# Graph rows as plain float32 of 256 columns in a graph block kernel

## The chip, the cores and the metric

The kernel runs on one core of a Trainium2 chip. The metric is the device time of one execution in microseconds. A core has five engines, each with its own queue of instructions, in order: TensorE (PE in the profile, with the loads of its stationary side shown as PEld), VectorE (DVE), ScalarE (ACT), GpSimd (POOL) and SyncE (SP, which here only issues DMA transfers). TensorE multiplies a stationary tile (up to 128 x 128) with a moving tile (up to 512 columns) into PSUM; VectorE and ScalarE read PSUM and write SBUF.

## The reference

There are 6250 nodes with 256 features and 200,000 edges sorted by destination. Cut to what matters here:

```
xn  = layernorm(x)
# graph convolution, with a self-loop for each node
h   = xn @ W
deg = number of edges into a node, plus 1;  dinv = 1 / sqrt(deg)
gnn = relu(segment_sum(h[src] * dinv[src] * dinv[dst], dst) + b)
# linear attention and a two-layer network on xn
mix = attention_block(xn)
x   = x + gnn + mix
# eight experts of 977 slots each, a token goes to its best expert
out = x + experts(layernorm(x))
```

The graph part can be written with rows g = dinv * h. For a node n it is relu(dinv[n] * (g[n] + the sum of g[s] over all edges s -> n) + b). The row g[n] is the self-loop, called the own row below.

## The kernel before

**Tiles.** The nodes lie in 49 tiles of 128 rows (the last has 106). The rows g of all 49 tiles are held in SBUF in `tabs` (`table`, `rows_of`, `source`, lines 128 to 145) and are also stored in DRAM as `g_dram`. Each row is kept in two parts of type float32r, 256 columns each: a first part written by ScalarE (`table_row`, line 475) and the rest, which VectorE computes as value minus first part (`table_rest`, line 481). So a row has 512 columns and 2 KB. float32r is float32 in size; TensorE multiplies it in another way than plain float32.

**First passes.** `first_passes` goes over pairs of tiles (`twos`), computes the normed x, its products and the attention's sums, and the rows g. Beside it `first_chain` searches in the sorted edges, finds degrees and builds the edge lists. Until the degrees are known (`dinv`), h is put back in the place of x (line 908); `late_rows` (line 485) turns these into rows g later, with `table_row` on ScalarE and `table_rest` on VectorE. `store_rows` (line 468) issues the transfers to `g_dram` on SP's queue. x is loaded at the start into SBUF that the tables take over later; from pair 20 on it is loaded a second time (`XIN`, line 60).

**The graph's sums** are made in two ways, each for a part of the 49 destination tiles.

- *Dense* (`dense`, line 1152), 32 tiles (`DTS`). For a destination tile u a matrix of edge counts A (source by destination, 49 blocks of 128 x 128) is built: VectorE makes one-hot rows (`onehots`, line 1134), TensorE multiplies them in bfloat16 (line 1177), ScalarE evicts the counts from PSUM into A as uint8 (lines 1181 and 1184). Then ScalarE widens five blocks of A at a time to float32r (`widened`, line 1165), and TensorE multiplies each block with the rows of its source tile into the PSUM tile `ps_d` (line 1199). This goes in 11 steps for a tile: the counts of tile u are built in the same steps in which those of tile u - 1 are multiplied (in steps 1 to 10, with 4 or 5 blocks each). There is one `ps_d`.
- *Gathered* (`gather`, line 1224), 17 tiles (`GTS`) with 33 groups of 128 edges each, 561 in all. GpSimd gathers the 128 source rows of a group from `g_dram` by an indirect DMA (line 1230), `LAG` = 7 groups ahead into `GB` = 9 buffers; VectorE makes a one-hot of the destinations (line 1245); TensorE multiplies it with the rows into `ps` (line 1256).

Edges that exceed the lists' room lie in one more tile of rows (`left`), which is added with a matmul for each destination tile (lines 1196 and 1255). The own row is added by a matmul of the identity with the row itself (lines 1195 and 1253), the first into its PSUM tile. At the end of a tile `put_sum` (ScalarE, line 1121) writes dinv times the first 256 columns, and `put_rest` (VectorE, line 1126) adds dinv times the other 256.

**Rounds.** `rounds` (line 1344) takes the pairs of tiles through the attention block, adds bias (`add_bias`, line 1384), the graph's sum and x, and does the routing. A finished pair is put into a slot tile (`to_slot`, line 1387; three buffers) and scattered to the experts' rows by GpSimd (line 1337).

**Order.** The three run as generators under an order written out by hand (lines 1704 to 1742): for each of 363 steps one step of `dense`, then steps of `rounds` and of `gather` at fixed rates. The order of instructions in each engine's queue is set by this and does not depend on times. After that the eight experts run (lines 1804 to 1838), in plain float32.

## Time and profile before

| | |
|---|---|
| three runs | 1502.11, 1503.97, 1504.27 us (median 1503.97) |
| the profiled execution | 1500.01 us |
| its span, first to last instruction | 1498.2 us |
| mean granted TensorE clock | 0.979 |
| TensorE busy | 1397.7 us (93%) |
| VectorE busy | 1004.2 us (67%) |
| ScalarE busy | 900.1 us (60%) |
| GpSimd busy | 745.3 us (50%) |
| DMA | 267.52 MB, mean 179 GB/s |

The page gives busy times over the span, then 40 equal slices of it with a digit for the busy share in tenths. A line of a group reads: source line, engine, operation, written tile <- read tiles, shapes, number of instructions | busy us, mean ns of one | idle time of the engine just before them, and who ended it. Busy time counts overlapping instructions once, so it can be less than number times mean. A line of a window reads: stretch, its length, busy time of each engine with the number of instructions, granted clock, DMA share and GB/s. A line of waits reads: who <- for whom: us in total, times, the longest. A line of the timeline reads: start, length, engine, group, number.

### The profile page before, as it was taken

How to read it: one execution, taken by the hardware profiler on the slowest of the kernel's cores; microseconds unless marked ns; L12 is line 12 of the kernel's file. 1: busy time of each engine (PE TensorE's matmuls, PEld its weight loads, DVE VectorE, ACT ScalarE, POOL GpSimd, SP SyncE). 2: the span in 40 equal slices, each digit the busy share in tenths (PEclk: the TensorE clock that was granted, in tenths of full speed). 3: DMA queues.
4: the chain of work that ended last, by engine and by line, in shares of the span. 5: the costliest groups of instructions: out<-in, count | busy, mean ns of one | idle time of the engine just before them, and what ended most of it. 6: DMA issues, size and time to landing. Idle time of an engine off the chain costs nothing. (4 is left out here: it accounts for less than half of the span.)

```text
span 1498.2 us, 22383 instructions
## 1 busy us (share of the span) xinstructions
PE 1397.7 (93%) x7002; PEld 1020.9 (68%) x7002; DVE 1004.2 (67%) x3435; ACT 900.1 (60%) x2051; POOL 745.3 (50%) x725
## 2 busy tenths in 40 slices
PE   5998997999998999999999989999997999999996
PEld 2665664777776777777776767767775767766854
DVE  6787696678887887878888878888865322222322
ACT  2776564677776777677776767777674333333321
POOL 0101542777776677777766677777661201111111
PEclk9999998999999999999999999999998999999998
DMA  8438675877787777877777777777765343333130
GB/s 266 144 124 275 195 233 172 225 198 201 188 219 207 180 201 211 223 200 214 204 202 205 196 192 202 186 209 210 182 170 171 120 149 110 127 129 132 47 109 11
DMA packets 173459, 267.52 MB, mean 179 GB/s; under 512 B 26409, under 2 KB 73984, under 8 KB 173318
## 3 DMA queue, kind: packets, MB, share of 16 engines
q0 software_dynamic: 89168, 166.39, 42.7%
q1 hardware_dynamic: 83268, 98.39, 19.9%
q10 hardware_dynamic: 882, 1.05, 0.3%
q8 instruction: 65, 1.06, 0.3%
q14 instruction: 76, 0.62, 0.1%
HBM read 208.05 MB, written 60.39 MB: 179 GB/s over the span
## 5 line engine op out<-in xcount | busy, mean ns | idle before, releaser
L1230 POOL DMA_INDIRECT gt<-g_dram,idxc x561 | 592.9, 1057 | 217.1 <-PE ps L1256 79.7
L1199 PE MATMUL ps_d<-tab,A_r 128*128 128x512 f32 x1568 | 425.8, 401 | 10.2 <-ACT A_r L1165 9.9
L1199 PEld LDWEIGHTS ps_d<-tab,A_r 128*128 128x128 f32 x1568 | 292.7, 190 | 88.6 <-ACT A_r L1165 26.5
L1181 ACT CAST A<-bp 128x294 uint8<-128x294 f32 x640 | 237.2, 430 | 186.9 <-PE bp L1177 185.4
L1165 ACT CAST A_r<-A 128x640 fp32r<-128x640 uint8 (+1 forms) x320 | 230.7, 723 | 6.6 <-PE ps_d L1199 5.0
L1256 PE MATMUL ps<-gt,oh 128*128 128x512 f32 x561 | 220.4, 451 | 2.5 <-DVE oh L1245 2.5
L1177 PE MATMUL bp<-hi,lo 128*128 128x147 bf16 x1408 | 187.3, 264 | 22.0 <-DVE hi L1134 13.1
L1177 PEld LDWEIGHTS <-lo 128*128 128x128 bf16 x1408 | 105.0, 105 | 123.0 <-issue 49.3
L1838 POOL DMA_INDIRECT out<-rep,who x43 | 42.5, 989 | 279.4 <-DVE rep L1835 225.5
L1804 PE MATMUL hpf<-xet,w1e 128*128 128x128 f32 (+3 forms) x576 | 159.2, 434 | 8.2 <-ACTq L1916 3.5
L1134 DVE TENSOR_TENSOR lo<-rowb,two 128x512 bf16<-128x512 bf16 x352 | 147.4, 419 | 21.0 <-PE bp L1177 13.6
L1134 DVE TENSOR_TENSOR hi<-hib,two 128x592 bf16<-128x592 bf16 x352 | 161.5, 459 | 0.0
L1814 PE MATMUL ypf<-w2e,hm 128*128 128x256 f32 (+1 forms) x688 | 151.4, 379 | 0.0
L1814 PEld LDWEIGHTS ypf<-w2e,hm 128*128 128x128 f32 (+1 forms) x688 | 128.8, 188 | 21.6 <-issue 2.6
L1245 DVE TENSOR_TENSOR oh<-rowb,rel 128x256 fp32r<-128x256 bf16 x281 | 116.2, 414 | 40.8 <-PE ps L1256 40.2
L1804 PEld LDWEIGHTS hpf<-xet,w1e 128*128 128x128 f32 x576 | 92.6, 198 | 66.4 <-issue 55.7
L1806 ACT ACTIVATE hm<-hpf,fb_s 128x128 f32<-128x128 f32 (+3 forms) x144 | 72.3, 513 | 87.6 <-PE hpf L1804 84.8
L1816 DVE TENSOR_TENSOR y<-ypf,fb_s 128x256 f32<-128x256 f32 (+1 forms) x43 | 18.2, 423 | 130.6 <-PE ypf L1814 130.6
L1256 PEld LDWEIGHTS ps<-gt,oh 128*128 128x128 f32 x561 | 97.2, 195 | 7.9 <-DVE oh L1245 3.4
L1817 ACT ACTIVATE y<-y,xe 128x256 f32<-128x256 f32 (+1 forms) x43 | 21.8, 508 | 124.8 <-DVE y L1816 124.8
L892 PE MATMUL mm<-wqkv_s,xnt 128*128 128x512 f32 (+1 forms) x196 | 93.4, 599 | 0.3 <-DVE tab L481 0.3
L1337 POOL DMA_INDIRECT xbuf<-slot,put x46 | 48.0, 1044 | 58.2 <-issue 29.5
(376 smaller groups left out, 1993.3 us busy)
## 6 DMA issues: line engine op xcount, KB each, us to landing
g_dram<-tab SPq DMA_DIRECT2D x24, 512.0 KB
xbuf<-zeros SPq DMA_DIRECT2D x26, 384.0 KB
gt<-g_dram,idxc POOLq DMA_INDIRECT x561, 3.8
w1e<-in_fw SPq DMA_DIRECT2D x8, 1024.0 KB
w2e<-in_fw SPq DMA_DIRECT2D x8, 1024.0 KB
xe<-xbuf SPq DMA_DIRECT2D x7, 1028.0 KB
xt<-in_x SPq DMA_DIRECT2D x28, 256.0 KB
xe<-xbuf SPq DMA_DIRECT2D x9, 771.0 KB
```

What stands on the lines that cost most here:

```text
L892: nc.tensor.matmul(kp[:r, :], xnt[:, c, i * r:i * r + r], wqkv_s[:, c, D:3 * D], start=(c == 0), stop=(c == 1))
L1134: V.tensor_tensor(one.rearrange("p g (w t) -> p g w t", t=2), row.rearrange("p (w t) -> p w t", t=2).unsqueeze(1).to_broadcast([P, 4, w // ...
L1165: nc.scalar.copy(o[:, :s1 - s0, :], mats[u][:, s0:s1, :])
L1177: nc.tensor.matmul(both[:, :, h * GN:(h + 1) * GN], lo[:, 2 * i + h, :], hi[:, 2 * i + h, :NB * GN].rearrange("p (s k) -> p s k", k=GN), s ...
L1181: nc.scalar.copy(mats[uu][:, :, GN * g:GN * (g + 2)], both)
L1199: nc.tensor.matmul(acc_ps, A[:, hi - s0, :], source(hi), start=False, stop=(hi == NB - 1))
L1230: nc.gpsimd.indirect_dma_start(out=gt, out_offset=None, in_=g_dram, in_offset=bass.IndirectOffsetOnAxis(ap=idxs[j // P][:, j % P:j % P + 1 ...
L1245: V.tensor_tensor(oh, rowb.unsqueeze(1).to_broadcast([P, 2, P]), rel[:, m:m + 2].unsqueeze(2).to_broadcast([P, 2, P]), op=OP.is_equal)
L1256: nc.tensor.matmul(ps, ohs.pop(i), tiles.pop(i), start=False, stop=(e == EB - 1))
L1804: nc.tensor.matmul(hp[:, :nn], w1e[:, c, f * P:(f + 1) * P], xet[:, c, at:at + nn], start=(c == 0), stop=(c == 1))
L1806: nc.scalar.activation(hm[:, f, :nn], hp[:, :nn], AF.Relu, bias=fb1_s[:, e * 8 + f:e * 8 + f + 1])
L1814: nc.tensor.matmul(yp[:r, :], hm[:, f, (i - i0) * P:(i - i0) * P + r], w2e[:, f, :], start=(f == 0), stop=(f == FF - 1))
```

## The change

Rows g are kept as plain float32 in one part of 256 columns. So `tabs` and `g_dram` have half the size and a gathered row has 1 KB. Every graph matmul takes plain float32 operands on both sides and 256 moving columns. ScalarE evicts the counts as float32, and the matmuls read them where they were written; `widened` goes. The identity matmuls go; `put_sum` is an addition by VectorE of the PSUM tile and the own row, for the dense tiles at the start of the next tile's first step, and the factor dinv moves into `add_bias`. `table_rest` goes; in `late_rows` the second tile of a pair is done by VectorE. The gather has 12 buffers and a lag of 9, the slots have 5 buffers, x is not loaded a second time, and the SBUF places of the tables and of x are dealt out anew. The path for inputs that do not fit the lists (under `flag == 1`) is changed likewise; it does not run on these inputs.

```diff
-GB = 9
-LAG = 7
+GB = 12
+LAG = 9
...
-XIN = 20
...
-    g_dram = dram.tile([N_NODES, 2 * D], F32, name="g_dram")
+    g_dram = dram.tile([N_NODES, D], F32, name="g_dram")
...
-            where = (3, 4, 5, 0, 1, 2, 6)[k]
-            tabs[k] = big.tile([P, min(8, NB - 8 * k), 2 * D], FR, name="tab", tag=f"T{where}")
+            where = (6, 0, 7, 1, 2, 3, 8)[k]
+            tabs[k] = big.tile([P, min(8, NB - 8 * k), D], F32, name="tab", tag=f"T{where}")
...
     def table_row(t, h):
 
         r = rows(t)
-        o = rows_of(t, 1)[:, 0, :]
-        nc.scalar.activation(o[:, :D], h, AF.Copy, scale=dinv[:r, t:t + 1])
-
-    def table_rest(t, h):
-
-        r = rows(t)
-        o = rows_of(t, 1)[:, 0, :]
-        V.scalar_tensor_tensor(o[:, D:], h, dinv[:r, t:t + 1], o[:, :D].bitcast(F32), op0=OP.mult, op1=OP.subtract)
+        nc.scalar.activation(rows_of(t, 1)[:, 0, :], h, AF.Copy, scale=dinv[:r, t:t + 1])
...
             for i in range(n):
-                table_row(t0 + i, x_in(t0 + i, 1)[:, 0, :])
-            yield
-            for i in range(n):
-                table_rest(t0 + i, x_in(t0 + i, 1)[:, 0, :])
+                t, h = t0 + i, x_in(t0 + i, 1)[:, 0, :]
+                if i:
+                    V.tensor_scalar(rows_of(t, 1)[:, 0, :], h, dinv[:, t:t + 1], None, op0=OP.mult)
+                else:
+                    table_row(t, h)
             store_rows(t0, n)
+            yield
...
-                if direct:
-                    table_rest(t0 + i, kp[:r, D:])
...
+    ma = tables.enter_context(tc.tile_pool(name="ma", bufs=2))
...
-            nc.scalar.activation(sums[gi][:r, t % 2, :], ps[:r, :D], AF.Copy, scale=dinv[:r, t:t + 1])
-
-        def put_rest(t, ps):
-            r = rows(t)
-            o = sums[t // 2][:r, t % 2, :]
-            V.scalar_tensor_tensor(o, ps[:r, D:], dinv[:r, t:t + 1], o, op0=OP.mult, op1=OP.add)
+            V.tensor_add(sums[gi][:r, t % 2, :], ps[:r], source(t)[:r])
             there.add(t)
...
-            def widened(u, p):
-
-                s0, s1 = share(p)
-                o = parts[p] = de.tile([P, 5, P], FR, name="A_r", tag="A_r")
-                nc.scalar.copy(o[:, :s1 - s0, :], mats[u][:, s0:s1, :])
...
                 for p in range(half):
+                    if rest is not None:
+                        put_sum(*rest)
+                        rest = None
                     if p == 1:
                         counted()
                     if u >= 1 and p >= 1:
 
                         if p == 1:
-                            acc_ps = dps.tile([P, 2 * D], F32, name="ps_d", tag="ps_d")
-                            nc.tensor.matmul(acc_ps, identr, source(DTS[u - 1]), start=True, stop=False)
-                            nc.tensor.matmul(acc_ps, ohl, left, start=False, stop=False)
-                        A, (s0, s1) = parts.pop(p), share(p)
-                        for hi in range(s0, s1):
-                            nc.tensor.matmul(acc_ps, A[:, hi - s0, :], source(hi), start=False, stop=(hi == NB - 1))
+                            acc_ps = dps.tile([P, D], F32, name="ps_d", tag="ps_d")
+                            nc.tensor.matmul(acc_ps, ohl, left, start=True, stop=False)
+                        for hi in range(*share(p)):
+                            nc.tensor.matmul(acc_ps, mats[u - 1][:, hi, :], source(hi), start=False, stop=(hi == NB - 1))
                     if u < ND:
                         if p == 0:
-                            mats[u] = de.tile([P, NB, P], U8, name="A", tag="A")
+                            mats[u] = ma.tile([P, NB, P], F32, name="A", tag="A")
...
-                    gt = tiles[j] = ga.tile([P, 2 * D], FR, name="gt", tag="gt")
+                    gt = tiles[j] = ga.tile([P, D], F32, name="gt", tag="gt")
...
-                    oh = ga.tile([P, 2, P], FR, name="oh", tag="oh", bufs=3)
+                    oh = ga.tile([P, 2, P], F32, name="oh", tag="oh", bufs=3)
...
-                        ps = gps.tile([P, 2 * D], F32, name="ps", tag="ps")
-                        nc.tensor.matmul(ps, identr, source(t), start=True, stop=False)
+                        ps = gps.tile([P, D], F32, name="ps", tag="ps")
...
-                    nc.tensor.matmul(ps, ohs.pop(i), tiles.pop(i), start=False, stop=(e == EB - 1))
+                    nc.tensor.matmul(ps, ohs.pop(i), tiles.pop(i), start=(e == 0), stop=(e == EB - 1))
...
-                V.tensor_add(sums[c][:r, :n, :], sums[c][:r, :n, :],
-                             gnn_b_s[:r].unsqueeze(1).to_broadcast([r, n, D]))
+                for i in range(n):
+                    o = sums[c][:r, i, :]
+                    V.scalar_tensor_tensor(o, o, dinv[:r, t0 + i:t0 + i + 1], gnn_b_s[:r], op0=OP.mult, op1=OP.add)
...
-                slot = slots[c] = rd.tile([P, 2, ROW], F32, name="slot", tag="slot", bufs=3)
+                slot = slots[c] = rd.tile([P, 2, ROW], F32, name="slot", tag="slot", bufs=5)
```

## The prediction

> **What bounds the kernel now.** I read the page's busy times and slices first, then three windows cut where the work changes, then TensorE's groups by shape, then its timeline at two places, and last what TensorE waited for.
>
> The page says that TensorE is busy almost everywhere and hardly throttled:
>
> ```profile
> PE 1397.7 (93%) x7002; PEld 1020.9 (68%) x7002; DVE 1004.2 (67%) x3435; ACT 900.1 (60%) x2051; POOL 745.3 (50%) x725
> PE   5998997999998999999999989999997999999996
> PEclk9999998999999999999999999999998999999998
> ```
>
> The first matmul on a graph row starts at 257 us and the last ends near 1146 us. So I cut the span into the passes before the graph (0 to 260), the graph with the rounds woven into it (260 to 1130), and the last rounds with the experts:
>
> ```profile
> core 0: us, PE busy (x) PEld busy (x) DVE busy (x) ACT busy (x) POOL busy (x), PEclk, DMA share, GB/s
> 0.00:260.00 260.00, 225.99 (x943) 149.22 (x944) 197.57 (x774) 150.63 (x390) 66.71 (x80) 0.96 0.64 202
> 260.00:1130.00 870.00, 835.61 (x4593) 623.93 (x4592) 690.88 (x2307) 629.17 (x1418) 626.38 (x593) 0.99 0.76 200
> 1130.00:1498.00 368.00, 336.06 (x1469) 247.76 (x1469) 115.78 (x355) 120.26 (x244) 52.24 (x52) 0.96 0.33 112
> ```
>
> In the middle stretch TensorE is idle for only 870.0 - 835.6 = 34.4 us. VectorE has 179 us of slack there, ScalarE 241, GpSimd 244, and the DMA engines are busy 76%. A change in this stretch is therefore worth what it does to TensorE's work, plus at most 34 us of waits. Matmul records overlap, so a busy TensorE could still have room; the starts in the timeline decide that. By shape the graph's two groups and two others are:
>
> ```profile
> L1199 PE MATMUL ps_d<-tab,A_r 128*128 128x512 f32 x1568 | 425.8, 401 | 10.2 <-ACT A_r L1165 9.9
> L1256 PE MATMUL ps<-gt,oh 128*128 128x512 f32 x561 | 220.4, 451 | 2.5 <-DVE oh L1245 2.5
> L1177 PE MATMUL bp<-hi,lo 128*128 128x147 bf16 x1408 | 187.3, 264 | 22.0 <-DVE hi L1134 13.1 <-ACT A L1184 5.1 <-ACT A L1181 3.2
> L1814 PE MATMUL ypf<-w2e,hm 128*128 128x256 f32 x656 | 144.5, 379 | 0.0
> ```
>
> The counts matter most. Dense work is 32 node tiles by 49 source tiles, 1568 matmuls, and L1199 has 1568 records: a float32r matmul leaves one. The experts' second product (L1814) is written with plain float32 operands, and the page has it 688 times with both forms, for 43 additions at L1816, each after 8 matmuls, that is 344 matmuls: a plain float32 matmul leaves **two** records, each with a weight load. Now what one record takes from the next, in the timeline (start, length, group, count):
>
> ```profile
> 602.11 1.31 PE L1199 MATMUL ps_d<-tab,A_r 128*128 128x512 f32 x5
> 603.27 0.51 PE L1177 MATMUL bp<-hi,lo 128*128 128x147 bf16 x4
> 603.56 0.70 PE L1256 MATMUL ps<-gt,oh 128*128 128x512 f32 x2
> 604.10 1.33 PE L1199 MATMUL ps_d<-tab,A_r 128*128 128x512 f32 x5
> ...
> 605.89 0.40 PE L1253 MATMUL ps<-tab,ident 128*128 128x512 f32 x1
> 606.12 0.39 PE L1256 MATMUL ps<-gt,oh 128*128 128x512 f32 x1
> ```
>
> ```profile
> 1303.80 13.98 PE L1814 MATMUL ypf<-w2e,hm 128*128 128x256 f32 x64
> 1317.61 0.60 PE L1793 MATMUL mm<-ident,xe 128*128 128x128 f32 x4
> ```
>
> Start to start, five float32r matmuls of 512 columns take 603.27 - 602.11 = 1.16 us, 0.232 each. In the experts 64 records of 256 float32 columns take 13.81 us, 0.216 each. Within the 1.99 us from 602.11 to 604.10 the three groups follow each other without a gap: TensorE is really full. What little it waits for in the middle stretch is this:
>
> ```profile
> PE ps_d L1199 <- ACT A_r L1165: 9.2, 13, 1.6
> PE ps L1255 <- DVE ohg L1242: 6.7, 5, 2.8
> PE bp L1177 <- DVE hi L1134: 5.1, 7, 1.3
> PE bp L1177 <- ACT A L1184: 5.1, 7, 1.1
> ```
>
> **The change, part by part.** *Graph matmuls (L1199, L1256, L1196, L1255).* 1568 + 561 + 32 + 17 = 2178 matmuls turn from one float32r record of 512 columns into plain float32 over 256 columns. L1814 has the same shape after the change (128x128 float32 weights, 256 float32 columns, sums kept in PSUM), so I take its price: two records of 0.216. The second record adds 2178 x 0.216 = 470 us; the first is shorter than before by 0.232 - 0.216 = 0.016, which is 35 us less. All of it is on TensorE in the stretch that TensorE fills. Bounds: if the 0.016 isn't saved, +470; if a gather matmul just after the counting matmuls (a lone one starts at 601.80 and the next group at 602.11, 0.31 against 0.232) shows its weight load twice, 352 steps x 0.08 = 28 more; on the low side, the busy time of both groups holds some half-clock stretches and hidden waits, which I put at 15 us.
>
> The row of 0.216 per record can be set against two rules of the Trainium skill. "FP8 and Floating Point Precision", section TensorE Precision Notes, counts four passes for true float32; "TensorE: Matmul & The Clock Gate", section Back-to-back issue gap, gives columns / 2.4 + 2.5 ns, so as an estimate 4 x 109 = 437 ns against 216 ns for 512 columns in one pass, or 2178 x 0.221 = +481 us. "Perfetto Trace Analysis", section Engine Utilization, only halves the output rate for FP32_LOW_HIGH; taken for the whole matmul that is 213 ns and no loss at all. L1814's two records per matmul side with the first, and the row, not the rule, goes into the sum.
>
> *Own row.* 49 identity matmuls go (L1195, L1253); one takes 606.12 - 605.89 = 0.23 us: -11 us on TensorE. In their place VectorE adds the row at eviction.
>
> *Casts and evictions.* ScalarE loses 320 casts of L1165 (230.7 us) and 49 copies of L1121 (0.47 each, 23 us); its 704 evictions of counts now write float32 in place of uint8. The page has 0.43 us for 294 columns to uint8, and L863 copies 512 float32 columns out of PSUM in 0.59, so I keep 0.43, bounded by 0.33 (L1184's 196 columns) and 0.59. Even 0.59 would add 113 us to an engine that has lost 254. TensorE's 9.2 us for A_r goes, since the matmul reads the counts where the eviction put them, a whole row tile earlier. VectorE loses 49 x 0.48 at L1126 (23.5) and gains 49 additions out of PSUM at 0.42 (L1816's row, 21 us) and, for 24 bias additions of 0.68, 49 multiply-adds at about 0.48: +7 us net beside 179 us of slack. The other 24 us of TensorE's waits are on VectorE and ScalarE, which get about 420 us more for less work: I take half, 12 us. Together -21, bounds 0 and -34.
>
> *A wait that is moved.* The dense sum is read by VectorE at the start of the next row tile's first step. There VectorE waits for the last dense matmul, and queued behind it are the one-hots (0.42 + 0.46) that TensorE needs one step later. Until then TensorE has two steps of counting and gather matmuls and the rounds' work, about 2.9 us at the new prices (two times 0.29 for counting, three gather matmuls at 0.43, some 1.0 of the rounds) against 1.3 us for addition and one-hots. I cost it at nothing; without that cover it would be up to 2 us for each of 32 tiles, 64 us.
>
> *Gather and DMA.* The 561 gathers keep their issue time on GpSimd (1.06 us each, 593 us in a stretch that will be near 1270) and fetch half the bytes; 12 buffers and a lag of 9 replace 9 and 7. GpSimd's waits there are mostly for TensorE to release a buffer. Nothing on TensorE's list waits for a gathered row, so this is worth 0, bounded by -2.
>
> *First passes.* 49 VectorE instructions of L481 go (23.5 us of 197.6), 11 ScalarE rows move to VectorE, the 25 stores by SP halve in bytes and five reloads of x go from SP's queue. TensorE is idle 34 us there, some 14 of it before 16 us, while the first loads land. Its wait of 2.8 us for begin_g at 132 us stands directly behind a run of L481: I take -3, bounds 0 and -9.
>
> *Experts.* Untouched; 5 slot buffers in place of 3 end a VectorE wait of 51.4 us that nothing on TensorE needs: 0, bounds -4 and +8.
>
> Sum: 470 - 35 - 11 - 21 - 3 = **+400 us** on the profiled execution's 1500.0 us, which is 1900. The median of the runs shown is 4 us above that execution, so the forecast for a median is 1904 us.
>
> **Rivals.**
> - *New waits on top.* One buffer for the dense sum and VectorE's wait in front of the one-hots stop TensorE at each row tile: +64, or the clock falls to 0.92 in a 1270 us stretch, about +90. Against it: the experts, float32 throughout, run at a granted clock of 1.00 from 1200 to 1400. Time 1940 to 2000.
> - *The second pass partly hidden.* TensorE's stretches between groups could be set by weight loads (190 ns each), so that second records fill gaps. For it: 0.31 after the counting matmuls. Against: 0.232 in runs of five, where 190 is covered. If all 561 gather matmuls hid half of theirs, -60: 1844.
> - *Not slower.* One mechanism: a float32 matmul of 256 columns here costs one record of 0.216, since its stationary side holds small whole numbers. Then 2178 x -0.016 - 11 - 21 - 3 = -70, about 1434 us. It decides once a matmul costs under 0.232 + 35/2178 = 0.248 us. Against it: L772 too has a stationary side of zeros and ones in float32, and the profile has 32 records for its 16 matmuls.
>
> **How the numbers follow.** Chances: forecast as summed 0.86, new waits 0.07, partly hidden 0.05, not slower 0.02. The first case's bounds are 1904 - 13 - 15 - 6 = 1870 and 1904 + 28 + 8 = 1940; it holds more than 8 in 10 by itself, so the range is 1870 to 1940. A measurement of this kernel tells about 0.2% from no change. Faster 0.015, same 0.005, slower 0.98.
>
> **What would show it.** L1199's and L1256's successors as 3136 and 1122 records of 256 columns, 0.216 apart in runs; no L1165 group; the middle stretch near 1270 us, with TensorE idle about 13 us; ScalarE and VectorE each busy about half of it; the stretches before and after within 10 us of now. Wrong would be: one record for each matmul, the middle stretch under 1230, or TensorE idle over 60 us there.

## The result and the profile after

The changed kernel takes 1833.97 us (median of 4 runs, 1832.55 to 1836.71), the kernel before 1503.04 (4 runs, 1500.41 to 1504.27). The ratio is 1.2207 [1.2182, 1.2231]: 331 us slower. The profiled execution took 1836.71 us with a span of 1834.9, against 1500.01 and 1498.2 before. Slower was forecast, by 400 us; the range began at 1870, 36 us above the measured time. Medians and ratios here and below leave out single executions more than 1.5% above the fastest of the same kernel.

The page after, busy times and slices:

```profile
PE 1780.4 (97%) x9131; PEld 1451.0 (79%) x9131; DVE 1009.6 (55%) x3421; ACT 679.1 (37%) x1671; POOL 714.9 (39%) x725
PE   6999989999999999999999999999999999999996
PEclk9999989999999999999999999999999998999998
```

TensorE has 9131 records in place of 7002 (+2129, that is 2178 second records less 49 identity matmuls), 383 us more busy time, and is the only engine near its limit: ScalarE has fallen from 60% to 37%, VectorE from 67% to 55%. The graph's groups and the counting matmuls beside them, from the groups of instructions:

```profile
L1162 PE MATMUL ps_d<-tab,A 128*128 128x256 f32 x3136 | 728.2, 379 | 0.0
L1215 PE MATMUL ps<-gt,oh 128*128 128x256 f32 x1122 | 307.9, 387 | 0.0
L1139 PE MATMUL bp<-hi,lo 128*128 128x147 bf16 x1408 | 181.0, 261 | 8.6 <-DVE hi L1102 5.3
```

L1162 is the old L1199, with 3136 records for its 1568 matmuls; L1215 is the old L1256, with 1122 for 561. Each plain float32 matmul leaves two records, as forecast. The timeline (start, length, group, count) gives their price:

```profile
250.45 0.64 PE L1215 MATMUL ps<-gt,oh 128*128 128x256 f32 x2
250.92 2.32 PE L1162 MATMUL ps_d<-tab,A 128*128 128x256 f32 x10
253.08 0.51 PE L1139 MATMUL bp<-hi,lo 128*128 128x147 bf16 x4
253.41 1.07 PE L1215 MATMUL ps<-gt,oh 128*128 128x256 f32 x4
```

Ten records take 253.08 - 250.92 = 2.16 us, 0.216 each, with no gap between the groups.

To see where the 331 us come from I cut both spans at the same two pieces of work, the first counting matmul and the last dense one. Before (columns as in the windows of the prediction):

```profile
0.00:248.40 248.40, 215.78 (x891) 142.22 (x892) 186.50 (x742) 141.65 (x367) 57.62 (x72) 0.98 0.63 200
248.40:1146.60 898.20, 857.72 (x4692) 639.52 (x4691) 711.25 (x2386) 647.15 (x1455) 639.65 (x606) 0.99 0.76 201
1146.60:1498.20 351.60, 324.17 (x1420) 239.16 (x1420) 106.47 (x308) 111.26 (x229) 48.06 (x48) 0.96 0.31 107
```

and after:

```profile
0.00:232.20 232.20, 210.31 (x890) 140.05 (x891) 170.40 (x704) 137.09 (x356) 55.37 (x72) 1.00 0.61 182
232.20:1482.10 1249.90, 1245.89 (x6813) 1070.54 (x6813) 732.35 (x2411) 431.14 (x1087) 611.53 (x606) 1.00 0.29 85
1482.10:1834.90 352.80, 324.18 (x1430) 240.43 (x1428) 106.83 (x308) 110.86 (x228) 48.03 (x48) 0.97 0.31 106
```

The first passes are 16.2 us shorter, the middle stretch 351.7 longer, the experts 1.2 longer. In the middle TensorE's busy time grows by 388.2 and its idle time falls from 40.5 to 4.0 us. I share out this time in two ways, both worked out from the trace's starts and ends. By ends: each record gets the time from the previous record's end (or its own start, if later) to its own end; the ends of matmuls are modelled, and where two groups meet this decides which of them gets the overlap. By starts: each record gets the time from its own start to the next record's start, as the prediction counted, taken at the median of all records of the group with the same groups in front and behind; what exceeds these medians (idle time, half clock, short waits) stands in a row of its own.

| TensorE in the middle stretch, us | by ends, before | after | difference | by starts, before | after | difference | forecast |
|---|---|---|---|---|---|---|---|
| dense matmuls | 378.1 | 676.9 | +298.8 | 367.8 | 677.8 | +310.0 | |
| gather matmuls | 138.0 | 248.7 | +110.7 | 171.3 | 250.7 | +79.4 | |
| those on `left` | 13.2 | 22.2 | +8.9 | 12.5 | 22.7 | +10.2 | |
| all graph matmuls | | | **+418.4** | | | **+399.6** | 470 - 35 = +435 |
| own row | 13.5 | 0 | **-13.5** | 15.3 | 0 | **-15.3** | -11 |
| counting matmuls | 137.8 | 125.9 | **-11.9** | 112.5 | 117.6 | **+5.1** | 0 |
| all other groups | 177.0 | 172.2 | **-4.8** | 164.6 | 172.2 | **+7.6** | 0 |
| idle | 40.5 | 4.0 | **-36.5** | | | | -21 |
| above the medians, idle time included | | | | 53.9 | 8.8 | **-45.0** | -21 |
| first passes (whole stretch) | 248.4 | 232.2 | **-16.2** | 248.4 | 232.2 | **-16.2** | -3 |
| experts (whole stretch) | 351.6 | 352.8 | **+1.2** | 351.6 | 352.8 | **+1.2** | 0 |

The bold terms add up to +336.7 by ends, the difference of the two spans, and to +337.0 by starts; the forecast's add up to +400. The two ways agree that the graph's matmuls grew by less than forecast. On the gather matmuls and on the work that the change does not touch they differ, even in sign, so by ends these rows show little. By starts, all rows down to the other groups together are +397.0 us of work at the median pace, where the forecast had +424.

What TensorE still waits for in the middle stretch after the change (who <- for whom: total, times, longest), the first four rows:

```profile
PE bp L1139 <- DVE hi L1102: 5.3, 1, 5.3
PE bp L1139 <- ACT A L1143: 1.6, 7, 0.7
PE bp L1139 <- ACT A L1146: 0.9, 2, 0.7
PE mm L1455 <- ACT x1t L1447: 0.7, 1, 0.7
```

The 5.3 us (`hi` is a one-hot) stand directly before the first counting matmul, at 232.2, and so belong to the first passes. The only other wait for a one-hot, 0.2 us, comes one step later; after that nothing of TensorE waits for `ps_d` or for a one-hot any more. The wait that the change moves is there, on VectorE only:

```profile
DVE ag L1094 <- PE ps_d L1162: 22.5, 19, 4.6
```

VectorE stands 22.5 us in front of the dense sum, some 1 us at a time (the 4.6 is a single one, at the last dense tile), and from the second step on none of TensorE's waits is for the sums or the one-hots that VectorE makes behind it.

### The profile page after: what moved, and what is told of

Read it like the earlier page. It is cut to its first block, busy times and chain, and to the rows that moved or that the text cites. A ratio compares the mean times of both kernels' runs of the same rounds, so it can differ in the third digit from the quotient of the medians.

```text
span 1834.9 us, 26236 instructions
## 1 busy us (share of the span) xinstructions
PE 1780.4 (97%) x9131; PEld 1451.0 (79%) x9131; DVE 1009.6 (55%) x3421; ACT 679.1 (37%) x1671; POOL 714.9 (39%) x725
## 3 DMA queue, kind: packets, MB, share of 16 engines
q0 software_dynamic: 35216, 92.73, 17.5%
q1 hardware_dynamic: 82180, 90.94, 15.3%
## 5 line engine op out<-in xcount | busy, mean ns | idle before, releaser
L1190 POOL DMA_INDIRECT gt<-g_dram,idxc x561 | 565.7, 1008 | 561.1 <-PE ps L1215 447.4
L1162 PE MATMUL ps_d<-tab,A 128*128 128x256 f32 x3136 | 728.2, 379 | 0.0
L1162 PEld LDWEIGHTS ps_d<-tab,A 128*128 128x128 f32 x3136 | 596.4, 190 | 80.3
L1143 ACT COPY A<-bp 128x294 f32<-128x294 f32 x640 | 228.9, 411 | 782.5 <-PE bp L1139 782.4
L1215 PE MATMUL ps<-gt,oh 128*128 128x256 f32 x1122 | 307.9, 387 | 0.0
L1205 DVE TENSOR_TENSOR oh<-rowb,rel 128x256 f32<-128x256 bf16 x281 | 117.7, 419 | 217.7 <-PE ps L1215 217.0
L1215 PEld LDWEIGHTS ps<-gt,oh 128*128 128x128 f32 x1122 | 194.3, 193 | 14.8
L1139 PE MATMUL bp<-hi,lo 128*128 128x147 bf16 x1408 | 181.0, 261 | 8.6 <-DVE hi L1102 5.3
L1139 PEld LDWEIGHTS <-lo 128*128 128x128 bf16 x1408 | 130.2, 105 | 61.9 <-issue 12.1
L1337 ACT ACTIVATE s<-s,nb,rs 128x256 f32<-128x256 f32 (+1 forms) x98 | 53.9, 604 | 17.1 <-DVE nb L1395 17.1
```

The source lines that it names most:

```text
L1139: nc.tensor.matmul(both[:, :, h * GN:(h + 1) * GN], lo[:, 2 * i + h, :], hi[:, 2 * i + h, :NB * GN].rearrange("p (s k) -> p s k", k=GN), s ...
L1143: nc.scalar.copy(mats[uu][:, :, GN * g:GN * (g + 2)], both)
L1162: nc.tensor.matmul(acc_ps, mats[u - 1][:, hi, :], source(hi), start=False, stop=(hi == NB - 1))
L1190: nc.gpsimd.indirect_dma_start(out=gt, out_offset=None, in_=g_dram, in_offset=bass.IndirectOffsetOnAxis(ap=idxs[j // P][:, j % P:j % P + 1 ...
L1205: V.tensor_tensor(oh, rowb.unsqueeze(1).to_broadcast([P, 2, P]), rel[:, m:m + 2].unsqueeze(2).to_broadcast([P, 2, P]), op=OP.is_equal)
L1215: nc.tensor.matmul(ps, ohs.pop(i), tiles.pop(i), start=(e == 0), stop=(e == EB - 1))
```

## The experiments

Four things were to be told apart. First, is it the second record that costs the time, or a new wait? Second, why did TensorE's waits vanish: because the casts are gone, because the gather is deeper, or because each step now holds more TensorE work than the other engines need? Third, what shortened the first passes by 16 us? Fourth, what does the own row on VectorE cost by itself? On four of the six chips used the kernel before took 1598 to 1612 us instead of 1502, so every ratio below is against the kernel before on the same chip. These four are called disturbed below.

**Both kernels as they are, on one more chip.** No edit.

> The kernel before, unchanged, for its trace on the chip of these runs, since beside the earlier runs it had 1599 to 1612 us in place of 1503. Theory A: the engines are stopped there now and then with nothing to wait for (as in the runs with one record, 4 to 5 us at a time on ScalarE), and TensorE, whose groups wait for ScalarE's evictions within one step, stands idle for some 80 us in the middle stretch in place of 34. Theory B: the gathers of 2 KB rows are slower there: then TensorE waits for gathered rows. If the chip is an undisturbed one: 1503 us and 34 us idle.

> The changed kernel, unchanged, beside the kernel before. Theory A: stops of 4 to 5 us fall into steps that are 1.4 times longer and in which TensorE has work left, so they are hidden: 1834 to 1852 us whatever the kernel before has, and TensorE is idle under 10 us in the middle stretch. Theory B: they are shared by both: some 100 us over 1834 where the kernel before is 100 us over 1503.

Measured: the kernel before 1502.39 us beside 1501.76; the changed kernel 1834.82, ratio 1.2208 [1.2176, 1.2240]. The first counting matmul starts at 250.0 and 232.7 us. So the 331 us and the 17 us of the first passes repeat.

**One record for a matmul.** The rows, the counts and the one-hots of the changed kernel are declared float32r, still with 256 columns:

```diff
+FR = mybir.dt.float32r
-            tabs[k] = big.tile([P, min(8, NB - 8 * k), D], F32, name="tab", tag=f"T{where}")
+            tabs[k] = big.tile([P, min(8, NB - 8 * k), D], FR, name="tab", tag=f"T{where}")
-                            mats[u] = ma.tile([P, NB, P], F32, name="A", tag="A")
+                            mats[u] = ma.tile([P, NB, P], FR, name="A", tag="A")
-                    gt = tiles[j] = ga.tile([P, D], F32, name="gt", tag="gt")
+                    gt = tiles[j] = ga.tile([P, D], FR, name="gt", tag="gt")
...
```

(likewise `oh`, `ohl`, `ohg`, `left`). It leaves out the second part of each row, so its sums are less exact than either kernel's.

> The changed kernel with rows, counts and one-hots as float32r of 256 columns, so that the second part of each row is left out and the graph sums lose accuracy. Theory A: the cost of the change is the second record of each of the 2178 graph matmuls. Then one record each, and a matmul takes 0.11 (half of 0.216, by columns) to 0.19 us (one weight load): TensorE's work in the middle stretch falls from 1246 to 530 to 710 us, VectorE with 702 us there becomes the bound, and the time is 1290 to 1400 us. Theory B: float32 matmuls are slow for another reason (reading 4-byte operands, or VectorE's eviction): then the time stays over 1500 us.

> The same kernel as the run with one record (float32r of 256 columns, second part of the rows left out), again, since in that run the engines stopped for 4 to 5 us some 60 times with nothing to wait for that the trace shows (ScalarE 251 us in all), and the kernel before had 1612 us beside it in place of 1503. There a float32r matmul of 256 columns took 0.12 us from the next in runs. Theory A (the second record is the cost): without such stops TensorE has some 600 to 650 us of work in the middle stretch and VectorE some 700, and the time is 1300 to 1400 us. Theory B (something else in the changed kernel costs it, such as VectorE's eviction or the counts in place): over 1500 us again.

> The changed kernel with float32r rows of 256 columns and no second part, again, for a chip on which the kernel before takes 1503 us. Theory A (the second record is the whole cost of the change): TensorE has 600 to 650 us of work in the middle stretch, VectorE 700, and the time is 1300 to 1420 us. Theory B: something else in the changed kernel holds it: over 1480 us.

> The changed kernel with float32r rows of 256 columns and no second part, for a chip on which the kernel before takes 1502 us (1568 to 1586 against 1599 to 1612 on three others, with ScalarE stopped for 200 to 250 us). Theory A (the second record is the whole cost of the change): 600 to 650 us of TensorE's work in the middle stretch, 1300 to 1420 us. Theory B (something else in the changed kernel holds it): over 1480 us.

Measured, on four chips: 1576.44, 1568.23, 1585.90 and 1566.56 us; ratios 0.9779 [0.9738, 0.9821], 0.9809 [0.9759, 0.9859], 0.9831 [0.9758, 0.9904], 0.9783 [0.9723, 0.9843]. Of the last one, groups, timeline, a window and two rows of waits:

```profile
L1163 PE MATMUL ps_d<-tab,A 128*128 128x256 f32 x1568 | 279.2, 316 | 0.0
```

```profile
464.06 0.76 PE L1163 MATMUL ps_d<-tab,A 128*128 128x256 f32 x5
464.66 0.51 PE L1140 MATMUL bp<-hi,lo 128*128 128x147 bf16 x4
```

```profile
260.00:1200.00 940.00, 685.88 (x4515) 605.54 (x4514) 688.77 (x2310) 421.45 (x1053) 651.03 (x587) 0.83 0.44 106
```

```profile
ACT A L1144 <- remote: 212.2, 55, 8.0
PE bp L1140 <- ACT A L1144: 92.4, 57, 6.6
```

With the type alone the records fall back to one for each matmul. On the two chips where versions of the changed kernel ran that keep two records (1848.05 and 1846.22 us, below), the time falls by 272 and 260 us. On the first of them TensorE's busy time between the first counting and the last dense matmul falls from 1247.3 us (nine buffers, below) to 705.4, and at the medians by starts the same work takes some 600 us in place of 1241. Together with the 4.0 us that TensorE is idle after the change, this shows that the matmuls in two records, not a new wait, are what the change costs. It does not price the second record alone, since the record that stays gets shorter too: five take 464.66 - 464.06 = 0.60 us, 0.12 each, where a matmul of two records takes 0.432.

The times alone do not decide it: all four lie above the 1480 or 1500 us that the expectations gave to another cause. The work that goes came out only in part, since waits took its place. Between the first counting and the last dense matmul TensorE is idle for 260 to 273 us in these four runs. In the window above it is busy 686 of 940 us, at a granted clock of 0.83, and the eviction of the counts stops 55 times, 212 us in all, where the trace names nothing of this core that it waits for ("remote"). What the stops are, and what this version takes on a chip without them, is not shown.

**The gather's depth.** The changed kernel with the old buffers:

```diff
-GB = 12
-LAG = 9
+GB = 9
+LAG = 7
```

> The changed kernel with 9 gather buffers and a lag of 7, as before, in place of 12 and 9. By both theories nothing on TensorE waits for a gathered row, so 1834 us within 3; it is also what the run with the casts is to be compared with. If the deeper gather mattered, TensorE would show waits for the gathered tile and the time would be over 1840.

Measured: 1848.05 us, 1.1457 [1.1409, 1.1505]. The cut middle stretch of this chip, beside the changed kernel as it is on the undisturbed one:

```profile
260.00:1465.00 1205.00, 1201.79 (x6587) 1031.94 (x6584) 700.92 (x2297) 415.48 (x1046) 588.04 (x588) 1.00 0.28 83
```

```profile
260.00:1465.00 1205.00, 1202.85 (x6594) 1033.24 (x6592) 701.39 (x2293) 416.22 (x1047) 587.34 (x581) 1.00 0.28 82
```

TensorE is idle 3.2 us with nine buffers and 2.2 with twelve, and waits for no gathered row in either. From the first counting to the last dense matmul it takes 1251.9 us with nine and 1249.8 with twelve. So depth is worth next to nothing, as forecast (0, bounded by -2), though the two stood on different chips. The 1848.05 us are more than the expectation allowed (1834 within 3); 8.7 of the 14 us more come before the first counting matmul (240.9 us in place of 232.2), where versions with twelve buffers are late on such chips too (236.6 to 237.5 with one record).

**The casts back in the changed kernel**, with the old depth:

```diff
+            def widened(u, p):
+                s0, s1 = share(p)
+                o = parts[p] = de.tile([P, 5, P], F32, name="A_r", tag="A_r")
+                nc.scalar.copy(o[:, :s1 - s0, :], mats[u][:, s0:s1, :])
...
-                        for hi in range(*share(p)):
-                            nc.tensor.matmul(acc_ps, mats[u - 1][:, hi, :], source(hi), start=False, stop=(hi == NB - 1))
+                        A, (s0, s1) = parts.pop(p), share(p)
+                        for hi in range(s0, s1):
+                            nc.tensor.matmul(acc_ps, A[:, hi - s0, :], source(hi), start=False, stop=(hi == NB - 1))
```

> The changed kernel, with ScalarE's 320 casts put back as copies from the float32 counts into a tile of five blocks that TensorE reads (9 gather buffers and a lag of 7 make room for it). ScalarE gets 230 us more work in the middle stretch, 416 to about 650 of 1250 us. Theory A: TensorE's waits in the middle stretch (40 us before, 4 after) went because ScalarE's cast no longer stands between the counts and the matmul. Then 9 us or more of waits for that tile return, with half-clock stretches behind them: 1844 to 1854 us. Theory B: they went because every step is 1.4 times longer, so that any engine is in time. Then under 3 us of such waits, full clock, and 1834 within 3 us.

> The changed kernel with ScalarE's 320 casts put back, again (1848 us beside 1848 for the changed kernel with 9 buffers, on a chip where the kernel before took 1612). Theory B of that run, longer steps put any engine in time: 1834 within 3 us and no wait of TensorE for the widened tile. Theory A, the cast stood in the way: 9 us or more of such waits, 1844 or more.

Measured: 1848.25 us, 1.1481 [1.1439, 1.1523], on the chip of the nine buffers (1848.05); 1846.22, 1.1472 [1.1429, 1.1515], on another. Both lie in the range that the expectation gave to waits for the cast, but the version with nine buffers alone does so too, so the waits have to decide. The window of the second:

```profile
260.00:1465.00 1205.00, 1201.77 (x6573) 1029.31 (x6572) 700.97 (x2296) 604.78 (x1349) 585.50 (x587) 1.00 0.28 83
```

ScalarE carries 189 us more than with nine buffers alone (604.78 against 415.48), and TensorE is as busy in this window (1201.77 against 1201.79). TensorE's wait for `A_r` is nearly gone, on the chip of the nine buffers

```profile
PE ps_d L1171 <- ACT A_r L1135: 0.5, 2, 0.3
```

and 0.2 us on the other. So the 9.2 us that TensorE waited for `A_r` before did not go because the cast went: they go with the cast in place, in steps that are 1249.9 / 898.2 = 1.4 times as long. The casts are not quite free: from the first counting to the last dense matmul it takes 1257.2 us on both chips, against 1251.9 with nine buffers alone.

**One more cast buffer in the kernel before**, the same question from the other side:

```diff
-GB = 9
-LAG = 7
+GB = 8
+LAG = 6
-                o = parts[p] = de.tile([P, 5, P], FR, name="A_r", tag="A_r")
+                o = parts[p] = de.tile([P, 5, P], FR, name="A_r", tag="A_r", bufs=3)
```

(the gather gives up one buffer to make room)

> The kernel before with a third buffer for the widened counts (8 gather buffers and a lag of 6 make room for it). Theory A: of the 40 us that TensorE waits in the middle stretch before, 9 us and the half-clock stretches behind them come from the casts being made too late for want of a buffer: 9 to 15 us less than the kernel before, and under 3 us of waits for the widened counts. Theory B: ScalarE is late because its queue is in order and it waits for the counting matmuls; a buffer changes nothing: within 3 us, with the waits as they were.

Measured: 1500.91 us, 0.9983 [0.9969, 0.9997]. TensorE's wait:

```profile
PE ps_d L1199 <- ACT A_r L1165: 11.2, 16, 1.5
```

It had been 9.2 us in 13 waits in the stretch that the prediction shows. A buffer doesn't remove it, so the cast is not late for want of room. What is left is its place in ScalarE's queue, behind the evictions; that is argued, not shown.

**The late rows.** At tile 24 both kernels turn the rows held back into rows g, for several pairs in one burst; in the kernel before VectorE's part of that stands in front of the lists that TensorE needs next. First the old burst with its VectorE half put back into the changed kernel, its result going to a spare tile:

```diff
             for i in range(n):
-                t, h = t0 + i, x_in(t0 + i, 1)[:, 0, :]
-                if i:
-                    V.tensor_scalar(rows_of(t, 1)[:, 0, :], h, dinv[:, t:t + 1], None, op0=OP.mult)
-                else:
-                    table_row(t, h)
+                table_row(t0 + i, x_in(t0 + i, 1)[:, 0, :])
+            yield
+            for i in range(n):
+                t, h = t0 + i, x_in(t0 + i, 1)[:, 0, :]
+                V.scalar_tensor_tensor(spare, h, dinv[:, t:t + 1], rows_of(t, 1)[:, 0, :], op0=OP.mult, op1=OP.subtract)
             store_rows(t0, n)
-            yield
```

> The changed kernel, with only the late rows done as in the kernel before: ScalarE makes the rows of both tiles of a pair, and VectorE then makes a second pass over each row (into a spare tile that nothing reads). Everything else is as changed: half-size tables and stores, no reload of x, no second parts for the other 27 tiles. Theory A: the graph part starts 16 us earlier after the change (first counting matmul at 232.2 instead of 248.4 us) because the burst of late rows between 117 and 132 us got lighter, and TensorE waited there and then ran at half clock. Then this run starts its first counting matmul 9 to 13 us later than the changed kernel, TensorE is busy about 24 to 26 of the 30 us from 120 to 150, and the time is about 1844 us. Theory B: the gain in the first passes comes from the smaller transfers and the reload of x that went. Then the start stays within 3 us of 232 and the time within 3 us of 1834.

> The changed kernel with the late rows done as before, again, beside an undisturbed kernel before. Theory A (the lighter burst of late rows starts the graph 16 us earlier): first counting matmul at 241 to 248 us in place of 232.2, TensorE busy 24 to 26 of the 30 us from 120 to 150 us, and 1843 to 1850 us. Theory B (smaller transfers, no reload): 232 within 3 us and 1834 within 3.

> The changed kernel with the late rows done as in the kernel before. The two earlier runs of it stood on chips where the kernel before took 1599 to 1612 us and the changed kernel with 9 buffers 1848; there it was 1867 to 1875 with the first counting matmul at 249.3 and 252.3 us. Theory A (the lighter burst of late rows is what starts the graph earlier): first counting matmul at 243 to 248 us in place of 232.2, the waits for begin_g and gat (2.8 and 2.2 us before) back, and 1845 to 1851 us. Theory B (half of it is from the smaller stores and the reload that went): 240 us and 1842.

> The changed kernel with the late rows done as before, for a chip on which the kernel before takes 1502 us (on three chips where it took 1599 to 1612 the first counting matmul came at 249 to 252 us with the late rows back and at 237 to 241 without, and the time was 1867 to 1875 against 1846 to 1848). Theory A (the lighter burst is the whole gain of the first passes): first counting matmul at 243 to 248 in place of 232.2, 1845 to 1855 us. Theory B (half from smaller stores and the reload that went): 240 and 1842.

Measured: 1875.24 us, 1.1620 [1.1579, 1.1660]; 1866.80, 1.1666 [1.1605, 1.1727]; 1872.22, 1.1650 [1.1601, 1.1698]; 1865.43, 1.1676 [1.1626, 1.1727]. On two of these chips other versions of the changed kernel took 1846 to 1848 us, so it is 26 to 27 us slower (these have the old depth of the gather, which is worth next to nothing). The expectations had 1834 and 9 to 21 us more for the edit, so all four runs came out above them. The stretch from 120 to 150 us shows it, the kernel before first, then the changed kernel, then the edit (the last of the four):

```profile
120.00:150.00 30.00, 23.95 (x96) 16.79 (x94) 21.19 (x92) 17.77 (x45) 7.53 (x7) 0.89 0.93 321
```

```profile
120.00:150.00 30.00, 29.93 (x149) 21.90 (x148) 18.95 (x86) 18.13 (x45) 13.84 (x14) 1.00 0.86 260
```

```profile
120.00:150.00 30.00, 22.21 (x84) 15.30 (x83) 17.85 (x78) 16.94 (x42) 4.14 (x5) 0.83 0.59 183
```

In 30 us TensorE does 96 records before, 149 after, and 84 with the edit; the clock is 0.89, 1.00 and 0.83. TensorE's waits in this place with the edit:

```profile
PE cr_ps L602 <- DVE begin_g L341: 3.0, 1, 3.0
PE mm L291 <- ACT s L833: 2.7, 1, 2.7
PE cr_ps L609 <- DVE gat L599: 1.8, 1, 1.8
```

The changed kernel has none of them. The kernel before has the first and the third (2.8 and 2.2 us), and of the second only 0.3 us, so the edit stops TensorE somewhat more than the burst that it stands for. The first counting matmul starts at 249.3 to 252.3 us with the edit. Without it, on the same chips, it starts at 240.9 (nine buffers), 237.3 (casts back) and 236.6 (one record) in place of 252.3, at 239.2 (casts back) and 237.2 (one record) in place of 250.5, and with one record at 236.6 in place of 249.3 and at 237.5 in place of 249.6: 11 to 16 us earlier.

The two traces of the kernels as they are show the place without an edit. The same two groups, the kernel before first, then the changed kernel:

```profile
119.81 1.03 PE L867 MATMUL kv_ps<-s,ek 128*128 128x257 f32 x4
141.91 1.88 PE L892 MATMUL mm<-wqkv_s,xnt 128*128 128x512 f32 x4
```

```profile
119.84 1.03 PE L845 MATMUL kv_ps<-s,ek 128*128 128x257 f32 x4
131.88 1.88 PE L869 MATMUL mm<-wqkv_s,xnt 128*128 128x512 f32 x4
```

They are level at 119.8 us and 10.0 us apart behind the burst. Of the other 6, 3.4 come bit by bit until 229.4 us, and 2.7 with the wait directly before the first counting matmul, which had been longer than the 5.3 us shown above:

```profile
PE bp L1177 <- DVE hi L1134: 7.9, 1, 7.9
```

Another part of the edit's cost follows at once. From the first counting to the first dense matmul it takes 270.9 - 249.6 = 21.3 us with the edit, and 21.0 to 22.2 on the other three chips, against 12.7 in the changed kernel as it is, 14.4 with nine buffers and 14.2 and 16.8 with the casts back. With one record, without the edit, it takes 16.3 to 20.3 us, so not all of it need belong to the edit; what holds these steps up was not taken apart.

Then the same in the kernel before. At tile 24 only the pairs below tile 16 are turned at once, and the rest goes beside the next tiles:

```diff
-                        all_of(late_rows())
+                        while held_back and held_back[0][0] < 16:
+                            some = held_back.pop(0)
+                            for i2 in range(some[1]):
+                                table_row(some[0] + i2, x_in(some[0] + i2, 1)[:, 0, :])
+                            for i2 in range(some[1]):
+                                table_rest(some[0] + i2, x_in(some[0] + i2, 1)[:, 0, :])
+                            store_rows(*some)
```

> The kernel before, with the burst of late rows cut: at tile 24 only the late rows of tiles 0 to 15 are forced, the rest follow one pair per step. Theory A (the burst stops TensorE around 128 to 136 us and brings 6.8 us at half clock): first counting matmul 3 to 8 us earlier than 248.4, and the time 3 to 8 us under the kernel before. Theory B: TensorE's wait there is for begin_g and gat, which come behind all late rows in any order: no change within 3 us, or some us slower, since the edge lists start later.

Measured: 1591.22 us, 0.9953 [0.9924, 0.9982]. The wait for `begin_g` is gone, though TensorE then waits 2.1 us for ScalarE's `xnt` in the same place. The first counting matmul starts at 248.4 us, against 252.1 in the next experiment, on the same chip, whose first passes are those of the kernel before. So half a per cent is to be had from the order alone, 4 us of it in the first passes: less than the 10 in the changed kernel, where VectorE's part of the rows is gone besides.

**The own row by VectorE in the kernel before:**

```diff
+            for h in range(2):
+                V.scalar_tensor_tensor(o, source(t)[:r, h * D:(h + 1) * D].bitcast(F32), dinv[:r, t:t + 1], o,
+                                       op0=OP.mult, op1=OP.add)
...
-                            nc.tensor.matmul(acc_ps, identr, source(DTS[u - 1]), start=True, stop=False)
-                            nc.tensor.matmul(acc_ps, ohl, left, start=False, stop=False)
+                            nc.tensor.matmul(acc_ps, ohl, left, start=True, stop=False)
...
-                        nc.tensor.matmul(ps, identr, source(t), start=True, stop=False)
```

Here VectorE needs two more passes over a tile, one for each part of the row.

> The kernel before (float32r, two parts) with one part of the change done alone: the 49 identity matmuls go, and VectorE adds both parts of the own row, times dinv, at eviction (98 multiply-adds of about 0.48 us, 47 us on an engine with 179 us of slack). Theory A: TensorE's work alone sets the time of the middle stretch: 13 us less, 1490 us. Theory B: at the prices before, VectorE is late often enough (24 us of TensorE's waits are on VectorE and ScalarE), so the longer eviction gives the gain back: 1500 to 1512 us, with more waits for one-hots.

> The kernel before with the 49 identity matmuls done by VectorE at eviction, again, for a chip on which the kernel before takes 1503 us (beside 1599 it was 1.1% slower). Theory A (TensorE's work alone counts): 1490 us. Theory B (VectorE's 47 us more of work come back as TensorE's waits): 1500 to 1515 us.

> The kernel before with the own row added by VectorE at eviction, for a chip on which the kernel before takes 1502 us (1.1% and 0.5% slower on two others). Theory A (TensorE's work alone counts): 1490 us. Theory B (VectorE's 47 us more come back as TensorE's waits for one-hots and for ScalarE): 1500 to 1515 us.

Measured: 1616.96 us, 1.0113 [1.0080, 1.0147]; 1616.03, 1.0054 [1.0006, 1.0102]; 1619.32, 1.0121 [1.0070, 1.0172]. 11 us less work for TensorE makes it 0.5 to 1.2% slower. The additions and one of TensorE's waits, in the last run:

```profile
L1128 DVE SCALAR_TENSOR_TENSOR ag<-tab,dinv,ag 128x256 f32<-128x256 f32 x96 | 46.6, 486 | 3.4
```

```profile
PE ps L1256 <- DVE ohg L1244: 12.1, 4, 4.9
```

98 passes (96 of full tiles) at 0.486 us are 48 us more in VectorE's queue, and TensorE stands 12.1 us for a one-hot that VectorE makes. On the first of the three chips this wait is 11.4 us, against 1.6 in the version with the late rows split. That VectorE's longer queue is what eats the 11 us and 9 to 19 more is the likeliest reading; TensorE's waits for ScalarE's counts are larger (21.9 us in the last run), and which of them belong to the move was not taken apart. All three chips were disturbed ones.

**The disturbed chips as an experiment of their own.** There the changed kernel's versions lose less to the kernel before: 1.146 to 1.148 against 1.221. The same window of the own-row kernel (first chip it ran on) and of the nine buffers says why:

```profile
260.00:1200.00 940.00, 835.64 (x4390) 615.18 (x4390) 716.68 (x2333) 611.98 (x1372) 600.39 (x580) 0.96 0.70 181
```

```profile
260.00:1200.00 940.00, 937.44 (x5133) 804.91 (x5131) 546.00 (x1777) 322.38 (x812) 458.93 (x459) 1.00 0.29 84
```

With one record for each matmul TensorE is idle for 104 us in this window; with two it is idle for 2.6. In the first, ScalarE's evictions stop for 57.9 us with nothing named:

```profile
ACT A L1184 <- remote: 57.9, 18, 6.1
```

With nine buffers the trace names four such stops in the whole middle stretch, 9.0 us. That the long TensorE steps hide others is argued, not shown.

## Why the prediction was right, and where it was not

The mechanism was as forecast: two records for each graph matmul, on the engine that fills the stretch, and no new wait. What failed are the steps that price what goes: the float32r matmul, TensorE's waits with the half clock, and the start of the graph. All three were put too low.

*Graph matmuls, two records of 0.216.* Right in kind and in the price of a record: 3136 and 1122 records, 0.216 apart. The term was +435 and measured +399.6 by starts, +418.4 by ends, with 15 us below as its bound. The step that failed is the price of the matmul that goes, 0.232 for each of 2178, read from runs of five dense matmuls. By starts a dense matmul had cost 367.8 / 1568 = 0.235 us, but a gather matmul 171.3 / 561 = 0.305. Behind another gather matmul it took 0.231; some 310 of the 561 stood first behind counting matmuls or another group, and took as a rule 0.31 to 0.33, such as this one, whose next group starts at 602.11:

```profile
601.80 0.48 PE L1256 MATMUL ps<-gt,oh 128*128 128x512 f32 x1
```

After the change the two records of such a matmul take 0.47 (250.45 to 250.92 above). So the change added 0.14 to a gather matmul and not 0.20: 33 us less for the 561. The prediction had seen the 0.31 and used it only for its upper bound. Part of the 33 is a matter of where groups meet, since the counting matmuls and the other groups, put at nothing, took 12.7 more by starts; the rest, some 20 us, is real by this count. What makes a first matmul slower is not shown.

The Trainium skill, "FP8 and Floating Point Precision", section TensorE Precision Notes, counts four passes for true float32; two records of 0.216 for 256 columns, 0.432 us, agree with it (the prediction's estimate from it was 0.437), and the rule in "Perfetto Trace Analysis", section Engine Utilization, that halves the rate does not, if it is taken for the whole matmul.

*Own row.* -15.3 by starts and -13.5 by ends against -11; the 49 matmuls went, 0.31 or 0.28 each and not 0.23. That VectorE's addition costs nothing held in the changed kernel. It does not hold everywhere: in the kernel before, the move loses 0.5 to 1.2%. The cover named in the prediction (steps of TensorE that are longer than VectorE's work) is the likely difference, which is argued; besides, that move needed 98 passes there and not 49.

*Casts and evictions, TensorE's waits.* The step was -21: all of A_r's 9.2 and half of the other 24. It measured -36.5, since nearly all idle time went. This is a failed step, and for A_r its reason failed too: with the casts back, and nearly as much work on ScalarE as before (605 us in a window of 1205, against 629 in one of 870), TensorE waits at most 0.5 us for them. So not the lighter ScalarE but the 40% longer step removes that wait. For the waits on VectorE the same is likely, though argued: VectorE has more work in the stretch than before (732 us, 711 before), and they are gone all the same. In all, 4 of 40 us are left. The prediction's +7 us net for VectorE is +5 by its own figures, which changes nothing.

*The clock, and work of TensorE that the change does not touch.* Both stood in the sum at nothing. Above the medians there were 53.9 us before, 40.5 of them idle, and 8.8 after, 4.0 of them idle; so 13.4 and 4.8 are neither work nor idle time. This fits the clock: the stretches at a granted clock of 0.5 came to 26.5 us in the middle stretch before and to 8.7 after, and half of such time is lost (in one of them, at 138.51 us in the kernel before, eight matmuls of L881 take 3.56 us; behind it, at 147.71, they take 1.89). So some 9 us came back with the waits, for which the sum had no term. The work that isn't touched fell by 16.7 us by ends and grew by 12.7 by starts, so a gain there is not shown.

*First passes.* Forecast -3, bounds 0 and -9; measured -16.2, 7 us outside the bounds. The step that failed is the wait for `begin_g`, priced at its own 2.8 us. Behind it came a second wait of 2.15 us and then 6.8 us at half the clock, which cost some 3.4, and before it small waits of 0.6: together 9.0 of the 10.0 us by which the two traces part here. The experiments agree that the burst of VectorE's work in front of them is the cause (11 to 16 us with a burst somewhat heavier, on other chips).

*The moved wait of `put_sum`.* Costed at nothing, with a cover of 2.9 us; VectorE waits 22.5 us and TensorE not at all. Right.

*Gather and DMA, experts.* 0 and 0; measured next to nothing for the depth, and +1.2 us. Right.

*Rivals.* New waits (1940 to 2000): none came. Not slower (one record, about 1434): excluded by the record count. The second pass partly hidden gave 1844, nearer to the time than the forecast. In runs of dense matmuls its mechanism does not hold, since records follow each other 0.216 apart. For the gather matmuls it names the right place, and its 60 us stand against the 33 above by starts (nothing by ends); that weight loads are the cause is not shown. Over half of the miss comes from waits, clock and first passes, of which it says nothing, so that its number lies near is in part luck.

So the 63 us by which the sum was too high are 27 (work at the median pace: 35 on the graph's matmuls and 4 on the own row, less 13 on other groups) + 15.5 (waits) + 8.6 (clock) + 13.2 (first passes) - 1.2 (experts). The bounds below covered 15 for the graph's matmuls, 13 for the waits and 6 for the first passes, 34 in all. The other 29, and 7 by which the medians lie otherwise to their profiled executions than the forecast took it, are the 36 us between range and time. Half of the miss and more (waits, clock and first passes, 37 us) is time that the kernel before lost because TensorE was not quite full, and a change that fills it gets that time back.

## What to carry to other kernels

Count a matmul's records before a type is changed: here plain float32 over 256 columns costs 0.432 us against 0.235 for float32r over 512 in runs of dense matmuls, and on an engine that is 95% busy nothing hides it. When a change makes one engine the clear bound, price what it replaces from start to start where it stands, a matmul that comes first behind another group apart from one in a run, and let nearly all of that engine's waits in the stretch go: here 36 of 40 us went. A wait of TensorE costs more than its own length where the clock drops behind it.

## What was not expected of the hardware

- A float32r matmul of 256 columns took 0.12 us, about half of the 0.232 with 512 columns, though each has a weight load that the profile shows with 0.19 us.
- A float32r matmul of 512 columns took 0.231 us behind another one and 0.31 to 0.33 as the first behind counting matmuls or another group.
- The granted clock falls to 0.5 in stretches of 3.4, 6.8, 10.2 or 13.7 us. The one of 6.8 us at 134.9 us in the kernel before starts at the end of TensorE's two waits of 2.85 and 2.15 us with 0.4 us of matmuls between them. The Trainium skill, "TensorE: Matmul & The Clock Gate", section What's actually happening, has a window of about 3.4 us, which the lengths agree with. It asks for an idle window of that length; here two shorter waits close together were enough, and at 821.0 us a stretch began behind a single wait of 2.02 us.
- The same 92.73 MB of GpSimd's transfers are packed otherwise by the type of the rows and of the tiles that receive them alone. From the page's queues (packets, MB, share of 16 engines), the changed kernel and then the version with one record:

```profile
q0 software_dynamic: 35216, 92.73, 17.5%
```

```profile
q0 software_dynamic: 89168, 92.73, 24.8%
```

  As float32 they go in 35,216 packets that take 0.175 x 1835 = 321 us of the engines' time, as float32r in 89,168 that take 0.248 x 1572 = 390 us.
